# Moving the sums, weightings, selects and score transpositions of a graph attention kernel to other steps of its order

## The chip, the cores and the metric

The kernel runs on one core of a Trainium2 chip. The metric is the time of one execution on the device, in microseconds (us). The time before the change is 5646.86 us, the median of three runs between 5633.02 and 5650.22 us. The traced execution is a run of its own with its own time.

## The reference

One layer of attention over a graph with 12500 nodes and 412500 edges, with a softmax over all edges and two layer norms behind it. Cut to what matters:

```python
h = x @ Wn + bn; q = x @ Wq + bq; k = x @ Wk + bk; v = x @ Wv + bv
eh = edge_attr_64 @ We + be
attn_in = concatenate([q[src], k[dst], eh], axis=-1)
hmid = leaky_relu(attn_in @ A1 + b1, 0.2)
scores = leaky_relu(hmid @ A2 + b2, 0.2)          # 8 heads
w = softmax(scores.mean(axis=-1), axis=0)         # over all edges
out = segment_sum(w[:, None] * v[dst], src, num_segments=12500)
y = gamma * layernorm(h + out) + beta
result = layernorm(x + y)
```

The edges come sorted by `dst`. The sums go by `src`, which is in no order.

## The kernel before

The first layer is folded into the tables, so that an edge's hidden row is a sum of a part by its `dst`, a part by its edge features and a part by its `src`. The work is in two halves that run at the same time for most of the kernel.

The first half, `make`, goes through 403 groups of 1024 edges in the order of `dst`. In each group PE makes the rows of all edges with one-hot matrices (`rows`, L932 and L939), ACT copies them out of PSUM (`evacuate`, L950 and L951), and POOL scatters them with indirect DMAs (L962) into a table in HBM that is sorted by blocks of `src`. DVE makes the one-hots (L852 to L872) and, with counts from PE (L881), the places of the rows (L902 to L915). Each group is cut into six pieces by `yield`.

The second half, `sums_of`, takes the table back in units of up to four blocks, at most 16 tiles of 128 edges. For each unit SP loads rows into `rt` (L1146, six buffers), PE transposes them and adds the `src` part (`hidden`, L1236 and L1246, one call for four tiles), ACT copies the result out of its bank (`copied`, L1257) and DVE makes the leaky Relu (`leaky`, L1261). PE multiplies by A2 (`scores`, L1272), ACT applies a Relu to z (`above_zero`, L1286), and PE transposes z (`heads`, L1298, the score transpositions). DVE adds the heads and takes maxima (`maxima`, from L1314), PE transposes the maximum (`maximum`, L1331), and DVE makes the reference of the softmax from it (`reference`, L1340 and L1341). ACT takes the exponentials (`weights`, L1350). For each four tiles DVE then makes one-hot selects (`select`, L1359, two buffers), ACT multiplies them by the weights (`weigh`, L1373, three buffers), and PE sums the rows with them (`add`, L1406, one PSUM bank `psm`). DVE adds the sum to the earlier one (`total`, L1423; L1416 in the first part), which SP had loaded (`before_it`, L1383), and SP stores it (`store`, L1435).

`hidden`, `scores` and `rows` take their banks from one ring of five PSUM banks (`bank`).

The order is written out by hand. `lags` gives each operation of a unit a step, counted from the unit's own start. A new unit starts every eight steps, so several units are in flight, and an operation at step 20 of one unit stands in the same step as one at step 12 of the next. `do` puts an operation into its step; within a step the calls stand in the order of the units, and those with `late=1` come last. `load_at` of the rows follows from `lead`, and from the last step of `add` of the unit that had the buffer before. The steps are emitted between the pieces of `make`; once no group is left, the steps that remain, those of the last units and of the closing norms, run alone. Each engine runs its own instructions in the order in which they are emitted, and waits by semaphores for the others.

Of the kernel before, what the change touches and what calls it, by code (L numbers as in the profile page):

```python
# [478 lines left out]
def sorted_path(  # L479
# [258 lines left out]
    above = const.tile([P, P], BF)  # L738
# [23 lines left out]
    late = {}  # L762
# [338 lines left out]
    def lags(p):  # L1101

        return dict(
            every=EVERY, lead=25 if p == NR - 1 else 19, sources=-13, turned=-12, spread=-7, q=-7,
            onehot=-2, copied=2, leaky=4, scores=12, above=14, heads=15, maxima=17, maximum=18,
            reference=20, weights=21, old=16, lowered=24, select=(19, 21, 23, 25),
            weigh=(21, 23, 25, 27), add=(24, 25, 27, 28), total=30, store=33,
        )

    def sums_of(bp):  # L1110


        plans, s0, free, starts, ends = [], 19, ([], []), {}, {}
        for p, bs, t in units:
            nt = len(bs) * t
            nk = -(-nt // 4)
            o = lags(p)
            if plans:
                s0 += plans[-1][4]["every"]


            mine = free[spare_buffer(len(plans))]
            held = MORE if mine is free[1] else BLKS
            load_at = mine[-held] + 1 if len(mine) >= held else 0
            s0 = max(s0, load_at + o["lead"] - 1)
            if plans:
                s0 = max(s0, plans[-1][2] + EVERY)
            if plans:
                s0 += (plans[0][2] - s0) % EVERY
            load_at = max(load_at, s0 - o["lead"])  # L1130
            mine.append(s0 + o["add"][-1])
            starts.setdefault(p, load_at)
            ends[p] = load_at
            plans.append((nt, nk, s0, load_at, o))
        steps = {}

        def do(step, fn, *args, late=0):
            steps.setdefault(max(int(step // 1), 0), []).append((late + step % 1, fn, args))
# [300 lines left out]
        def pieces(i):  # L1439
            at = list(range(0, plans[i][0], 4)) + [plans[i][0]]  # L1440
            return list(zip(at[:-1], at[1:]))

        for i, (nt, nk, s0, load_at, o) in enumerate(plans):
            do(load_at, load, i)
            do(s0 + o["sources"], sources, i)
            do(s0 + o["turned"], turned, i)
            do(s0 + o["turned"], put, i)
            do(s0 + o["spread"], spread, i)
            do(s0 + o["q"], load_q, i)
            for k, (c, c1) in enumerate(pieces(i)):  # L1450
                n, s = c1 - c, s0 + 2 * k
                t = units[i][2]
                for u in range(-(-c // t), (c1 - 1) // t + 1):
                    do(s + o["onehot"], onehot, i, u)
                do(s, hidden, i, c, c, n, k)
                do(s + o["copied"], copied, i, c, c, n, k, late=1)
                do(s + o["leaky"], leaky, i, c, c, n, k, late=1)
            do(s0 + o["scores"], scores, i, 0, nt)
            do(s0 + o["above"], above_zero, i)
            do(s0 + o["heads"], heads, i, 0, nt)  # L1460
            do(s0 + o["maxima"], maxima, i)
            do(s0 + o["maximum"], maximum, i, late=1)
            do(s0 + o["reference"], reference, i)
            do(s0 + o["weights"], weights, i)
            do(s0 + o["old"], before_it, i)
            do(s0 + o["lowered"], lowered, i)
            for j, t0 in enumerate(range(0, nt, 4)):
                n = min(4, nt - t0)
                if t0 % SEL == 0:
                    m = min(SEL, nt - t0)  # L1470
                    do(s0 + o["select"][j], select, i, t0, m)
                do(s0 + o["weigh"][j], weigh, i, t0, n)
                do(s0 + o["add"][j], add, i, t0, n)
            do(s0 + o["total"], total, i)
            do(s0 + o["store"], store, i)
# [350 lines left out]
    with tc.manual_schedule():  # L1826
# [6 lines left out]
        tabs, made, nt = tables(), 0, 1 + (2 * ng - 1) * (10 + 6) + ng  # L1833
        more, sent, ne = later(), 0, 11 * (len(chunks) - 1)
        done, r = 0, 0
        for i, _ in enumerate(_ for p in range(NP) for _ in make(p)):
            while fills and fills[-1][0] <= i:
                fill_piece(*fills.pop()[1])
            while made < nt and made * n0 < i * nt:
                next(tabs, None)  # L1840
                made += 1
            while sent < ne and sent * n0 < i * ne:
                next(more, None)
                sent += 1
            if i == n1:
                for _ in tabs:
                    pass
                for _ in more:
                    pass
                spans()  # L1850
                covered()
                tab_pool.close()
                steps, starts = sums_of(pool("blk", BLKS))
            if i < n1:
                continue
            while r + 1 < NR and i >= 6 * begun[r + 1]:
                r += 1
            if r + 1 < NR:
                until = starts[r] + (starts[r + 1] - starts[r]) * (i - 6 * begun[r]) / (
                    6 * (begun[r + 1] - begun[r])  # L1860
                )
                while done < until:
                    for fn, args in steps[done]:
                        fn(*args)
                    done += 1
# [86 lines left out]
```

## Time and profile before

| | |
|---|---|
| median of three runs | 5646.86 us |
| traced execution | 5660.61 us, span 5658.8 us |
| PE busy | 4277.5 us (76%) |
| DVE busy | 4078.5 us (72%) |
| POOL busy | 3455.8 us (61%) |
| ACT busy | 3104.1 us (55%) |
| moved by DMA | 1486.96 MB, 263 GB/s |
| mean granted TensorE clock | 0.832 |

PEld is the load of weights into PE, which runs beside its matmuls. "Issue" as the end of a wait means that the trace shows nothing that the engine waited for, "remote" that a semaphore was raised by something that the trace doesn't tell. An arrow says what ended a wait: "PE psS L1298 <- ACT z L1286" is PE, idle ahead of its transpositions at line 1298, until ACT's z of line 1286 was done. The ends of matmuls are modelled.

### The profile page before, as it was taken

The numbers are of one execution on the slowest core, as the hardware profiler recorded it, in microseconds if no ns is written. First come the engines' busy times: TensorE is split into PE (matmuls) and PEld (weight loads), VectorE is DVE, ScalarE is ACT, GpSimd is POOL, SyncE is SP. The second block draws the span as 40 slices with busy tenths as digits, with TensorE's granted clock in tenths as the row PEclk, the third lists the DMA queues.
The fourth block names the chain that finished last, engine by engine and source line by source line (L and its number), as shares of the span: only waits on it lengthen the run. The fifth ranks groups of instructions, "written<-read, shape, count | busy, mean of one in ns | idle before, by whom it ended". The sixth has DMA issues, their size and how long they took to land. (4 is left out here: it accounts for less than half of the span.)

```text
span 5658.8 us, 89624 instructions
## 1 busy us (share of the span) xinstructions
PE 4277.5 (76%) x28928; PEld 3043.3 (54%) x28928; DVE 4078.5 (72%) x8952; ACT 3104.1 (55%) x8846; POOL 3455.8 (61%) x3277
## 2 busy tenths in 40 slices
PE   4545536777778877778788887888777787888897
PEld 2333324555555565555555565656555555555677
DVE  7867745666667777767677777777777777776787
ACT  2432224444556566555555665666655666555786
POOL 4776666666666655666666666666556666666113
PEclk6766657778888888888888988888888889888999
DMA  6877866677777788877778888788887888887985
GB/s 189 275 255 255 251 221 207 225 236 233 242 267 275 261 276 270 263 273 257 263 267 283 293 270 289 274 273 272 273 266 268 271 283 275 272 276 254 351 318 188
DMA packets 727112, 1486.96 MB, mean 263 GB/s; under 512 B 157377, under 2 KB 326356, under 8 KB 724839
## 3 DMA queue, kind: packets, MB, share of 16 engines
q1 hardware_dynamic: 535538, 1055.66, 57.1%
q0 software_dynamic: 154752, 424.43, 20.5%
q10 hardware_dynamic: 36340, 1.05, 0.4%
q8 instruction: 229, 3.75, 0.3%
q14 instruction: 253, 2.06, 0.1%
HBM read 901.45 MB, written 579.32 MB: 262 GB/s over the span
## 5 line engine op out<-in xcount | busy, mean ns | idle before, releaser
L962 POOL DMA_INDIRECT rtab<-rec,idx x3224 | 3371.3, 1046 | 1866.2 <-issue 860.4
L950 ACT ACTIVATE rec<-bank 128x512 f32<-128x512 f32 x1612 | 882.5, 594 | 1195.3 <-remote 404.6
L1406 PE MATMUL psm<-rt,ohw 128*128 128x128 f32 x7448 | 1211.4, 307 | 158.3 <-issue 145.5
L1373 ACT ACTIVATE ohw<-ohs,w 128x128 f32<-128x128 bf16 x3724 | 1217.4, 403 | 44.9 <-DVE ohs L1359 17.9
L1406 PEld LDWEIGHTS psm<-rt,ohw 128*128 128x128 f32 x7448 | 1064.5, 215 | 238.8 <-issue 189.1
L1257 ACT ACTIVATE hm<-bank 128x512 f32<-128x512 f32 x932 | 550.7, 591 | 569.6 <-remote 125.5
L939 PE MATMUL bank<-WeS,eat 64*128 64x128 f32 x6448 | 748.4, 335 | 117.7 <-issue 113.9
L932 PE MATMUL bank<-kvs,ohd 128*128 128x256 bf16 x3224 | 591.1, 302 | 260.4 <-ACT rec L950 121.1
L902 DVE TENSOR_TENSOR ats<-pc,oh 128x792 f32<-128x792 f32 x403 | 393.0, 975 | 528.0 <-remote 235.3
L1236 PE MATMUL bank<-ident,rt 128*128 128x128 f32 x3724 | 673.7, 302 | 90.2 <-issue 85.9
L939 PEld LDWEIGHTS bank<-WeS,eat 64*128 64x128 f32 x6448 | 540.7, 216 | 357.6 <-issue 350.3
L1236 PEld LDWEIGHTS bank<-ident,rt 128*128 128x128 f32 x3724 | 467.8, 154 | 370.5 <-issue 282.6
L1246 PE MATMUL bank<-ohT,qs 128*128 128x512 bf16 (+3 forms) x2156 | 622.1, 380 | 57.5 <-issue 43.4
L1224 DVE TENSOR_SCALAR ohT<-rowB,iotaP,power 128x512 bf16<-128x512 uint8 (+1 forms) x980 | 563.4, 578 | 138.4 <-remote 47.1
L1261 DVE SCALAR_TENSOR_TENSOR hm<-hm 128x512 f32<-128x512 f32 x932 | 636.4, 683 | 3.5 <-ACT hm L1257 2.3
L872 DVE TENSOR_SCALAR ohd<-dstb,node 128x1152 bf16<-128x1152 uint8 x404 | 566.1, 1401 | 26.5 <-remote 19.4
L932 PEld LDWEIGHTS <-ohd 128*128 128x128 bf16 x3224 | 333.2, 107 | 440.7 <-issue 345.1
L1359 DVE TENSOR_TENSOR ohs<-iotaE,sl 128x512 bf16<-128x512 bf16 x932 | 394.4, 423 | 34.6 <-ACT ohw L1373 27.1
L1272 PE MATMUL bank<-hm,A2s 128*32 128x512 f32 x1864 | 385.4, 687 | 31.4 <-issue 22.3
L913 DVE TENSOR_REDUCE pos<-ats 128x8 f32<-128x792 f32 x403 | 390.1, 968 | 2.6
L1286 ACT ACTIVATE z<-bank,b_c 128x512 f32<-128x512 f32 (+3 forms) x252 | 170.7, 677 | 336.4 <-remote 224.8
L1298 PE MATMUL psS<-ident,z 128*128 128x128 f32 (+2 forms) x1000 | 183.7, 315 | 200.3 <-ACT z L1286 194.5
(198 smaller groups left out, 3760.7 us busy)
## 6 DMA issues: line engine op xcount, KB each, us to landing
rt<-rtab SPq DMA_DIRECT2D x192, 2056.0 KB
eat<-in_ea SPq DMA_DIRECT2D x201, 512.0 KB
rt<-rtab SPq DMA_DIRECT2D x48, 1542.0 KB
qs<-qtab SPq DMA_DIRECT2D x240, 256.0 KB
atab<-old SPq DMA_DIRECT2D x240, 256.0 KB
old<-atab SPq DMA_DIRECT2D x216, 256.0 KB
rtab<-rec,idx POOLq DMA_INDIRECT x3224
dstb<-dtab SPq DMA_DIRECT2D x201, 256.0 KB
```

The source lines that it names most:

```text
L872: nc.vector.tensor_scalar(to, row[:, cols], node, None, op0=ALU.is_equal)
L932: nc.tensor.matmul(pk[h][:, i, :], ohd[h * (GT // 2) + j + i], kvs, start=(i == 0), stop=False,)
L939: nc.tensor.matmul(pk[h][:, i, :D], eat[half, (j + i) * P : (j + i + 1) * P], WeS[half, :], start=False, stop=(i == 1),)
L950: nc.scalar.activation(rec[:, h, :, : 2 * D], pk[h], AF.Copy)
L962: one_tile = nc.gpsimd.indirect_dma_start(out=rtab[:, :], out_offset=bass.IndirectOffsetOnAxis(ap=idxs[g][:, t : t + 1], axis=0), in_=rec[ ...
L1224: nc.vector.tensor_scalar(st["oh"][u][:, : t * P].rearrange("p (t q e) -> p t q e", q=4, e=32), st["rowB"][:, : nt * P] .rearrange("p (q t ...
L1236: nc.tensor.matmul(ph[:, j * P : (j + 1) * P], st["rt"][:, t0 + j, :D], ident, is_transpose=True, start=(j == 0), stop=False,)
L1246: nc.tensor.matmul(ph[:, cols], st["qs"][:, u, s, :], st["oh"][u][:, (j0 - u * t) * P : (j1 - u * t) * P], start=False, stop=(s == 1 and j ...
L1257: nc.scalar.activation(hm, state[i].pop(("ph", k))[:, : n * P], AF.Copy)
L1261: nc.vector.scalar_tensor_tensor(hm, hm, SLOPE, hm, op0=ALU.mult, op1=ALU.max)
L1373: nc.scalar.activation(ohw[:, j, :], ohs[:, :, t0 % SEL + j], AF.Copy, scale=st["w"][:, t0 + j : t0 + j + 1])
L1406: nc.tensor.matmul(st["psm"][:, u * P : (u + 1) * P], ohw[:, j, :], st["rt"][:, t0 + j, D : 2 * D], start=(k == 0), stop=(k == t - 1),)
```

## The change

Only steps are changed; every operation stays as it is, and the same instructions are issued.

```diff
-            onehot=-2, copied=2, leaky=4, scores=12, above=14, heads=15, maxima=17, maximum=18,
-            reference=20, weights=21, old=16, lowered=24, select=(19, 21, 23, 25),
-            weigh=(21, 23, 25, 27), add=(24, 25, 27, 28), total=30, store=33,
+            onehot=-2, copied=2, leaky=4, scores=11, above=13, heads=15, maxima=17, maximum=18,
+            reference=20, weights=21, old=15, lowered=24, select=(19, 20, 22, 23),
+            weigh=(21, 22, 24, 25), add=(23, 25, 26, 27), total=29, store=32,
...
-            do(s0 + o["heads"], heads, i, 0, nt)
+            do(s0 + o["heads"], heads, i, 0, nt, late=1)
```

Scores, Relu, old sums, totals and stores go one step forward. The second select and weighting go one step forward, the third one, the last two. Of the sums the first, third and fourth go one step forward and the second stays. The transpositions stay in their step but come last in it.

What that does to the order of PE shows in the middle of the program, behind the last `hidden` of a unit. Before:

```order
L1246 MATMUL bank_41595<-ohT_41528,qs_41201 128x512
L1298 MATMUL psS_41614<-ident_81,z_41593 128x128 x4
L881 LDWEIGHTS above_276
L881 MATMUL pc_33945<-few_41588,above_276 128x99
L881 LDWEIGHTS above_276
L881 MATMUL pc_33945<-few_41588,above_276 128x99
L1406 MATMUL psm_41638<-rt_40365,ohw_41540 128x128 x4
L1236 MATMUL bank_41645<-ident_81,rt_41076 128x128 x4
```

With the change, at the same place:

```order
L1246 MATMUL bank_41602<-ohT_41530,qs_41206 128x512
L1406 MATMUL psm_41614<-rt_40368,ohw_41543 128x128 x4
L1298 MATMUL psS_41623<-ident_81,z_41548 128x128 x4
L881 LDWEIGHTS above_276
L881 MATMUL pc_33947<-few_41591,above_276 128x99
L881 LDWEIGHTS above_276
L881 MATMUL pc_33947<-few_41591,above_276 128x99
L1236 MATMUL bank_41653<-ident_81,rt_41079 128x128 x4
```

The first sum of the unit before (L1406, the first to write its `psm`) stood behind the transpositions (L1298) and the counts of `make`, and stands ahead of them now.

On ACT, around the weights of one unit and the Relu z of the next. Before:

```order
L1350 ACTIVATE w_28354,sums_353<-S_28232,ref_351 128x16
L1373 ACTIVATE ohw_28356<-ohs_28277,w_28354 128x128 x4
L950 ACTIVATE rec_28365<-bank_28306 128x2x256
L950 ACTIVATE rec_28365<-bank_28307 128x2x256
L951 ACTIVATE rec_28365<-srcl_210 128x4
L1286 ACTIVATE z_28380<-bank_28333,b2_c_110 128x512
L1257 ACTIVATE hm_28345<-bank_28338 128x512
L1373 ACTIVATE ohw_28406<-ohs_28361,w_28354 128x128 x4
```

With the change:

```order
L1350 ACTIVATE w_28357,sums_353<-S_28237,ref_351 128x16
L1373 ACTIVATE ohw_28359<-ohs_28281,w_28357 128x128 x4
L1286 ACTIVATE z_28364<-bank_28283,b2_c_110 128x512
L950 ACTIVATE rec_28368<-bank_28315 128x2x256
L950 ACTIVATE rec_28368<-bank_28316 128x2x256
L951 ACTIVATE rec_28368<-srcl_210 128x4
L1373 ACTIVATE ohw_28382<-ohs_28338,w_28357 128x128 x4
L1257 ACTIVATE hm_28347<-bank_28340 128x512
```

The Relu moved past the copies of a record, and the second weighting (the second L1373) past the copy of a hidden bank (L1257).

On DVE, from the reference of a unit on. Before:

```order
L1341 SCALAR_TENSOR_TENSOR ref_351<-m1_44432,ref_351 128x1
L1261 SCALAR_TENSOR_TENSOR hm_44340<-hm_44340 128x512
L1359 TENSOR_TENSOR ohs_44462<-iotaE_88,sl_43613 128x512
L852 TENSOR_TENSOR oh_44485<-blk_209,iotaE_88 128x792
L862 TENSOR_TENSOR both_44487<-oh_44485 128x396
L864 TENSOR_TENSOR few_44489<-both_44487 128x198
L872 TENSOR_SCALAR ohd_44491<-dstb_43913,node_269 128x3x384
L1423 SCALAR_TENSOR_TENSOR old_44136<-old_44136,by_44321,psm_44324 128x512
L1224 TENSOR_SCALAR ohT_44496<-rowB_44375,iotaP_90,power_206 128x384
L1224 TENSOR_SCALAR ohT_44498<-rowB_44375,iotaP_90,power_206 128x384
L1261 SCALAR_TENSOR_TENSOR hm_44398<-hm_44398 128x512
L1359 TENSOR_TENSOR ohs_44507<-iotaE_88,sl_43613 128x512
```

With the change:

```order
L1341 SCALAR_TENSOR_TENSOR ref_351<-m1_44436,ref_351 128x1
L1359 TENSOR_TENSOR ohs_44439<-iotaE_88,sl_43617 128x512
L1261 SCALAR_TENSOR_TENSOR hm_44346<-hm_44346 128x512
L1423 SCALAR_TENSOR_TENSOR old_44128<-old_44128,by_44329,psm_44316 128x512
L852 TENSOR_TENSOR oh_44488<-blk_209,iotaE_88 128x792
L862 TENSOR_TENSOR both_44490<-oh_44488 128x396
L864 TENSOR_TENSOR few_44492<-both_44490 128x198
L872 TENSOR_SCALAR ohd_44494<-dstb_43920,node_269 128x3x384
L1359 TENSOR_TENSOR ohs_44501<-iotaE_88,sl_43617 128x512
L1224 TENSOR_SCALAR ohT_44503<-rowB_44375,iotaP_90,power_206 128x384
L1224 TENSOR_SCALAR ohT_44505<-rowB_44375,iotaP_90,power_206 128x384
L1261 SCALAR_TENSOR_TENSOR hm_44402<-hm_44402 128x512
```

The second select (the first L1359) moved past a leaky Relu (L1261), the total (L1423) past the one-hots of a record group (L852 to L872), and the third select past two one-hots (L1224) and a leaky Relu.

## The prediction

> **What bounds the kernel now.** I read the page first, then busy time by stage, then who waits for whom inside the long middle stage, and last the instructions of one disturbed and one smooth stretch in order of time. The stages (busy us and instructions of PE, PEld, DVE, ACT and POOL, then granted clock, DMA share, GB/s):
>
> ```profile
> span 5658.8 us, 89624 instructions
> ...
> 0.00:900.00 900.00, 450.64 (x2473) 302.52 (x2473) 619.11 (x1074) 261.68 (x504) 590.72 (x570) 0.66 0.75 239
> 900.00:5190.00 4290.00, 3429.71 (x23469) 2423.71 (x23469) 3104.54 (x6817) 2492.36 (x7285) 2749.29 (x2636) 0.85 0.79 266
> 5190.00:5659.00 469.00, 397.10 (x2998) 317.07 (x2994) 354.89 (x1062) 350.05 (x1059) 115.75 (x73) 0.96 0.76 281
> ```
>
> The middle stage, where records are made and summed at once, is 4290 of 5659 us, and no engine fills it: PE is busy for 80% of it and DVE for 72%. In the tail PE is busy for 85%, ahead of DVE and ACT. The waits of the middle stage on PE, in us, times and longest, and one of DVE:
>
> ```profile
> PE psS L1298 <- ACT z L1286: 183.3, 88, 6.9
> PE psm L1406 <- issue: 144.6, 268, 1.5
> PE bank L939 <- issue: 112.0, 196, 1.3
> PE bank L1236 <- issue: 72.5, 136, 1.7
> PE bank L932 <- issue: 69.0, 101, 3.2
> PE bank L932 <- ACT rec L950: 51.7, 36, 5.4
> ...
> PE psm L1406 <- DVE old L1423: 4.1, 5, 1.3
> ...
> PE psm L1406 <- ACT ohw L1373: 3.2, 6, 0.9
> ...
> DVE ohs L1359 <- ACT ohw L1373: 16.6, 27, 1.4
> ```
>
> The largest single wait of PE is for the Relu z, ahead of the score transpositions (L1298): 88 times, 2.1 us each on average. Sums never wait for their weightings to speak of (3.2 us), so starting the weightings sooner can save nothing by itself. The four "issue" rows, 398 us, have no releaser and nothing in the change touches them. Now a disturbed stretch and the smooth one behind it, first by busy time of the same engines, then by instruction:
>
> ```profile
> 3490.00:3500.00 10.00, 2.97 (x18) 1.70 (x17) 2.29 (x5) 1.64 (x5) 6.24 (x7) 0.89 0.53 155
> 3500.00:3510.00 10.00, 9.56 (x69) 8.48 (x73) 9.76 (x25) 9.20 (x29) 4.76 (x4) 0.77 0.95 352
> 3510.00:3520.00 10.00, 10.00 (x89) 7.35 (x90) 9.83 (x22) 8.88 (x26) 8.17 (x7) 1.00 0.90 297
> ```
>
> ```profile
> 3487.24 1.06 PE L1272 MATMUL bank<-hm,A2s 128*32 128x512 f32 x8
> ...
> 3499.70 0.69 ACT L1286 ACTIVATE z<-bank,b_c 128x512 f32<-128x512 f32 x1 [7.17 <-remote]
> ...
> 3500.44 1.11 PE L1298 MATMUL psS<-ident,z 128*128 128x128 f32 x4 [3.37 <-ACT z L1286]
> ...
> 3508.50 0.16 DVE L1341 SCALAR_TENSOR_TENSOR ref<-m,ref 128x1 f32<-128x1 f32 x1
> ...
> 3509.55 0.30 ACT L1350 ACTIVATE w<-S,ref 128x16 f32<-128x16 f32 x1
> ...
> 3509.90 1.06 PE L1272 MATMUL bank<-hm,A2s 128*32 128x512 f32 x8
> 3509.97 1.33 ACT L1373 ACTIVATE ohw<-ohs,w 128x128 f32<-128x128 bf16 x4
> ...
> 3510.87 0.73 DVE L1423 SCALAR_TENSOR_TENSOR old<-old,by,psm 128x512 f32<-128x512 f32 x1
> ...
> 3511.21 0.66 ACT L1286 ACTIVATE z<-bank,b_c 128x512 f32<-128x512 f32 x1
> ...
> 3515.20 0.61 PE L1298 MATMUL psS<-ident,z 128*128 128x128 f32 x4
> ...
> 3515.65 1.06 PE L1406 MATMUL psm<-rt,ohw 128*128 128x128 f32 x8
> ...
> 3516.17 0.42 DVE L1359 TENSOR_TENSOR ohs<-iotaE,sl 128x512 bf16<-128x512 bf16 x1
> ...
> 3522.55 1.07 PE L1272 MATMUL bank<-hm,A2s 128*32 128x512 f32 x8
> ```
>
> The kernel runs in two modes. Undisturbed, a unit of eight steps takes 3522.55 - 3509.90 = 12.65 us with PE and DVE both full, and the transpositions find z ready 3.3 us early. Disturbed, DVE and ACT stand still for want of PE's results: the scores' matmuls at 3487.24 show an end at 3488.3, but z starts only at 3499.70 although ACT had been idle for 7.17 us, and PE, having done what it could, stands before the transpositions for 3.37 us. The waits for z belong to the second mode.
>
> **The change part by part.** Nothing is added or removed; work is moved.
>
> *The first sum ahead of the transpositions.* A sum of four tiles (1.06 us, row 3515.65) now stands before the transpositions and not behind them. When PE must wait for z, it does this sum first, if the partial sums' bank is free, and that seldom fails (L1406 <- DVE old, 4.1 us). Upper bound: 88 x 1.06 = 93 us. Lower bound: nothing, where another engine decides. Right after the wait at 3500.44 DVE is busy for 9.76 and 9.83 of 10 us, so a microsecond that PE saves there need not move the end; elsewhere PE is the fuller one. I take a third of the bound, -31 us. Between the scores and the transpositions nothing else is gained: scores and Relu both go one step forward, so that ACT gets z in the same order behind the first weighting.
>
> *The tail.* The same wait there:
>
> ```profile
> PE psS L1298 <- ACT z L1286: 11.2, 21, 1.7
> ```
>
> Its mean of 0.53 us is below one sum of 1.06 us, so nearly all of it is covered; at most -11.2 us. PE is the fullest engine there and I take -8.
>
> *Selects nearer to the weightings.* There are two select buffers, and the third and fourth select now follow the first and second weighting by one step instead of two. In the smooth stretch the reference ends at 3508.66 on DVE, and the first weighting on ACT at 3511.30. Behind the reference DVE would do a select (0.42), a total (0.73), and the one-hot and leaky Relu of
>
> ```profile
> 3508.58 0.54 DVE L1224 TENSOR_SCALAR ohT<-rowB,iotaP,power 128x512 bf16<-128x512 uint8 x1
> ...
> 3509.04 0.68 DVE L1261 SCALAR_TENSOR_TENSOR hm<-hm 128x512 f32<-128x512 f32 x1
> ```
>
> together 2.4 us, to 3511.0: without record work between, DVE stands for 0.3 us. Today's wait is 16.6 us in 27 waits, 0.61 each. Bounds: 0, and two selects in each of 220 units at 0.61, +268 us of DVE. I take three times today's, +33 us on DVE, a third of it on the path: +11 us.
>
> *The copy behind the second weighting.* The middle stage has 220 units, and 2632 / 8 = 329 groups of records:
>
> ```profile
> L932 PE MATMUL bank<-kvs,ohd 128*128 128x256 bf16 x2632 | 461.5, 292 | 148.1 <-issue 69.0 <-ACT rec L950 51.7 <-ACT hm L1257 11.6
> ...
> L1286 ACT ACTIVATE z<-bank,b_c 128x512 f32<-128x512 f32 (+2 forms) x220 | 149.1, 678 | 326.5 <-remote 224.8 <-PE bank L1246 51.2 <-PE bank L939 23.6
> ```
>
> On ACT the weights and first weighting (3509.55 to 3511.30), the Relu (0.66) and the second weighting (1.33) now follow each other, 3.7 us ahead of a copy that gives back one of five PSUM banks. One copy gets a weighting of 1.33 us ahead of it, another loses one. Bounds: +293 us, if all 220 units pay one weighting, and -63 us, if all that PE waits at L932 for record and hidden copies today (51.7 and 11.6) went. I take 0, between them, since the weightings ahead of copies are as many as before.
>
> *Totals, stores and loads.* Total, store and the load of the old sums move with the sums by one step. The total passes record work on DVE in some places, and it waits for a sum that moved as far; I take 0. On SP the order of row loads, stores and spreads stays, only record loads pass them. The place of the row load in the program does not move, and its buffer comes free at the same place of PE's order (the last sum stands just before the scores in both). 0, and the wait of the sums for rows, which the rows above do not show, stays hidden.
>
> Sum: -31 - 8 + 11 = -28 us. The profiled execution took 5660.6 us, its span 5658.8 and 1.8 around it; 5660.6 - 28 = 5632.6. It lies 13.7 us above the median of the runs, 5646.9, so for a median I predict 5646.9 - 28 = **5619 us**.
>
> **The rivals.**
>
> *No change.* The wait for z is a symptom: PE's late results hold up every engine, and when PE has done its sum it waits as long for the next thing that ACT or DVE has not done, since both resume only when the results arrive. For it: z at 3499.70 started 11.4 us after the recorded end of the scores, and one sum is 1.06 us. Against it: 88 waits of 2.1 us are twice a sum, not ten times. It leaves the tail's part and part of the select's cost, about -2: 5645 us. The Trainium skill, "Perfetto Trace Analysis", section "Summary: the profiler window per engine type", says that the end shown for TensorE is an estimate and that semaphore propagation lies outside the window; the 11.4 us between scores and z agree that the shown end is not when the consumer is let go.
>
> *Slower: ACT's burst holds the banks.* The 3.7 us of weights, weighting, Relu and weighting, and a record copy when one falls in, stand ahead of a copy of a hidden bank. A unit takes four hidden banks, one for scores and, with 1.5 groups of four, six for records; in a smooth stretch PE then asks for one every 12.65 / 11 = 1.15 us, five last for 5.8 us, and PE stands before L932 or L1236. If half of the 220 units lose half a weighting, 0.66 us, that is +73 on the path less the 39 saved: 5647 + 34 = 5681 us. It decides from the point where PE's waits for ACT at those lines rise by over 39 us. For it: ACT fills 8.88 and 9.20 of 10 us in smooth stretches. Against it: three of four copies stand behind a weighting today as well.
>
> *Faster still: the clock.* The clock drops when PE stands:
>
> ```profile
> 3497.00:3499.00 2.00, 0.07 (x1) 0.00 (x0) 0.56 (x2) 0.00 (x0) 1.01 (x1) 0.70 0.95 238
> 3499.00:3501.00 2.00, 0.56 (x3) 0.56 (x4) 1.15 (x2) 1.30 (x3) 0.00 (x0) 0.50 0.96 356
> 3501.00:3505.00 4.00, 4.00 (x20) 3.63 (x19) 3.83 (x12) 3.97 (x14) 0.67 (x1) 0.55 1.02 408
> ```
>
> Of 6 us after that wait, PE ran at about half its clock, some 2.7 us lost. If the sum that fills the wait keeps the clock up in 20 of the 88 cases, 54 us more are saved: 5619 - 54 = 5565 us. The Trainium skill, "TensorE: Matmul & The Clock Gate", section "What's actually happening", has the clock halve after an idle window of about 3.4 us; the 0.50 behind 3.37 us of waiting agrees. Against it: a pause that comes from late results is as long with the sum done first, only 1.06 us of it is filled.
>
> **How the numbers follow.** Forecast 0.38 (its own range 5595 to 5632), no change 0.30, slower 0.20, clock 0.12. The range for 8 in 10 reaches below to the clock's 5565, with a little of the 93 us bound beyond it, and above past the slower rival's 5681: 5558 to 5692. This kernel's runs tell 0.3% from no change, 17 us: faster is under 5630, slower over 5664. The clock and nearly all of the forecast are faster, 0.48; no change and the forecast's upper edge 0.31; the slower rival with a little of the upper edge of no change 0.21.
>
> **What would show it.** In the changed kernel's waits of 900 to 5190 us, L1298 <- z should fall from 183 us to some 100, and in the tail from 11 to under 3. L1359 <- ohw on DVE should rise from 16.6 to about 50; over 100 would say that the selects cost more than I gave them. L932 and L1236 <- ACT should stay near 64 us; 39 more and the slower rival is right. If z's wait falls but the time stays and waits at other lines of PE or the "issue" rows rise by as much, it was a symptom. If z's wait does not fall at all, the step about the first sum is wrong.

## The result, and the profile after

The changed kernel takes 5691.66 us (median of five runs, 5683.19 to 5708.17) against 5646.86 us of the kernel before (now five runs, the same median): a ratio of 1.0088, 95% interval 1.0064 to 1.0113. It is slower by 45 us between the medians, where a time 28 us shorter was forecast. The profiled execution has a span of 5689.9 us against 5658.8, 31 us more.

Busy time by stage in the profile after (us of the stretch, busy us and instructions of PE, PEld, DVE, ACT and POOL, granted clock, DMA share, GB/s):

```profile
span 5689.9 us, 89962 instructions
...
900.00:5190.00 4290.00, 3427.59 (x23402) 2411.20 (x23402) 3099.62 (x6798) 2468.35 (x7261) 2728.90 (x2630) 0.86 0.80 265
```

In the same 4290 us PE issues 23402 matmuls where it issued 23469, 0.3% fewer, and it stands for 862.4 us where it stood for 860.3. DVE stands for 1190.4, before 1185.5. So the idle time in these 4290 us is what it was, though the 0.3% of work not done in them would take some 12 us more. The waits are not what they were. Two rows of PE before that the prediction doesn't show, from 900 to 5190 us, in us, times and longest:

```profile
PE bank L932 <- ACT hm L1257: 11.6, 9, 2.3
PE bank L932 <- ACT z L1286: 8.7, 3, 3.7
```

After:

```profile
PE psS L1298 <- ACT z L1286: 1.7, 2, 0.8
...
PE bank L932 <- ACT z L1286: 74.8, 46, 5.5
PE bank L932 <- ACT rec L950: 68.4, 35, 5.8
PE bank L932 <- ACT hm L1257: 21.2, 21, 3.1
...
DVE ohs L1359 <- ACT ohw L1373: 132.9, 91, 5.8
```

The wait for z ahead of the transpositions, 183.3 us before, is gone. PE now stands at the next thing that it needs from ACT, the banks at L932 (z 8.7 to 74.8 us, records 51.7 to 68.4, hidden copies 11.6 to 21.2), and DVE stands at its selects (16.6 to 132.9). On DVE the groups of two lines show the same shift (busy us and mean ns, then idle time ahead of them and what ended it). Before, then after:

```profile
L902 DVE TENSOR_TENSOR ats<-pc,oh 128x792 f32<-128x792 f32 x330 | 321.9, 976 | 417.5 <-remote 167.9 <-PE psm L1406 53.6 <-PE psS L1298 44.6
...
L1340 DVE TENSOR_REDUCE m<-psS 128x1 f32<-128x128 f32 x218 | 61.0, 280 | 273.1 <-PE psm L1406 128.3 <-remote 65.6 <-PE bank L1272 29.0
```

```profile
L902 DVE TENSOR_TENSOR ats<-pc,oh 128x792 f32<-128x792 f32 x328 | 319.9, 975 | 306.8 <-remote 128.4 <-PE bank L939 47.6 <-PE psm L1406 35.7
...
L1340 DVE TENSOR_REDUCE m<-psS 128x1 f32<-128x128 f32 x216 | 61.0, 282 | 396.8 <-remote 105.3 <-PE bank L939 64.5 <-PE bank L1272 54.8
```

DVE waits 111 us less for the counts of the records and 124 us more for the maximum. From the 60th to the last group of records, by the places that DVE makes at L913, the two traces differ by 16 us (4451.0 and 4467.0). That is about half of the 31 us between the two spans, and single traces don't tell whether it is the change.

The tail is another matter, and has the other half. Its 25 units, the last part (from the weights, L1350, of unit 225 to those of unit 249), before and after:

```profile
5299.00:5524.00 225.00, 208.62 (x1588) 158.31 (x1587) 185.14 (x481) 198.44 (x612) 25.53 (x12) 1.00 0.89 331
```

```profile
5313.00:5554.00 241.00, 217.50 (x1588) 169.13 (x1586) 188.76 (x480) 198.32 (x612) 25.35 (x12) 0.99 0.87 308
```

The same instructions and the same 74 MB (331 GB/s in 225 us, 308 in 241) take 16 us longer, with no engine nearer to being full. What differs is SP. Its waits from 5300 to 5550 us, before and after:

```profile
SPq L1383 <- DMA atab<-old: 25.8, 15, 3.6
SPq L1383 <- DMA row<-slT: 25.8, 6, 5.5
SPq L1146 <- DMA rt<-rtab: 9.9, 5, 3.0
```

```profile
SPq L1383 <- DMA atab<-old: 104.8, 22, 7.8
```

SP waits 104.8 us for stores of the sums to land before it may load the next old sums (L1383) into their buffer, of which there are three. What stands behind that load shows in SP's instructions in order of time (start, duration, line). Before:

```profile
5386.56 0.42 SPq L1146 DMA_DIRECT2D rt<-rtab  x1
5393.19 0.33 SPq L1496 DMA_DIRECT2D end<-in_x  x1
5393.63 0.38 SPq L1383 DMA_DIRECT2D old<-atab  x1
5394.05 0.43 SPq L1435 DMA_DIRECT2D atab<-old  x1
5394.52 0.43 SPq L1214 DMA_DIRECT2D rowB<-row  x1
5395.05 0.62 SPq L1172 DMA_DIRECT2D qs<-qtab  x1
5395.72 0.70 SPq L1146 DMA_DIRECT2D rt<-rtab  x1
```

After:

```profile
5402.65 0.32 SPq L1504 DMA_DIRECT2D xtab<-end  x1
5408.36 0.32 SPq L1383 DMA_DIRECT2D old<-atab  x1
5408.73 0.43 SPq L1146 DMA_DIRECT2D rt<-rtab  x1
5409.97 0.33 SPq L1496 DMA_DIRECT2D end<-in_x  x1
5410.35 1.54 SPq L1435 DMA_DIRECT2D atab<-old  x1
5411.94 0.45 SPq L1214 DMA_DIRECT2D rowB<-row  x1
5412.49 0.51 SPq L1172 DMA_DIRECT2D qs<-qtab  x1
5420.92 0.32 SPq L1383 DMA_DIRECT2D old<-atab  x1
5421.30 0.43 SPq L1146 DMA_DIRECT2D rt<-rtab  x1
```

Before, the row load of 2 MB (L1146) is issued, and the load of the old sums waits behind it, with the rows under way. After, the load of the old sums stands ahead of the row load: SP stops from 5403.0 to 5408.4, and from 5413.0 to 5420.9, and only then issues the rows. The loads of `qs` and `rowB` come later too, and PE in the tail now waits for `qs` (L1246 on PEld, 3.8 us before):

```profile
PEld L1246 <- DMA qs<-qtab: 20.5, 14, 3.8
PE bank L1246 <- DVE ohT L1224: 12.8, 7, 3.9
```

The table of lags says why the order turned over. In the last part the row load's lead is 25, so it falls into step 7 of eight; `old` at 16 fell into step 0 behind it, and `old` at 15 falls into the same step 7, where an older unit's calls stand first. In the other parts the lead is 19.

### The profile page after: what moved, and what is told of

Same layout as the page of the kernel before. It is cut to its first block, busy times and chain, and to the rows that moved or that the text cites. A ratio compares the mean times of both kernels' runs of the same rounds, so it can differ in the third digit from the quotient of the medians.

```text
span 5689.9 us, 89962 instructions
## 1 busy us (share of the span) xinstructions
PE 4298.5 (76%) x28928; PEld 3048.2 (54%) x28928; DVE 4090.9 (72%) x8952; ACT 3086.9 (54%) x8846; POOL 3439.6 (60%) x3277
## 3 DMA queue, kind: packets, MB, share of 16 engines
q8 instruction: 229, 3.75, 0.3%
## 5 line engine op out<-in xcount | busy, mean ns | idle before, releaser
L950 ACT ACTIVATE rec<-bank 128x512 f32<-128x512 f32 x1612 | 879.5, 593 | 1212.8 <-remote 364.8
L1406 PE MATMUL psm<-rt,ohw 128*128 128x128 f32 x7448 | 1220.2, 309 | 210.6 <-issue 163.0
L1373 ACT ACTIVATE ohw<-ohs,w 128x128 f32<-128x128 bf16 x3724 | 1214.1, 399 | 75.3 <-remote 43.5
L1406 PEld LDWEIGHTS psm<-rt,ohw 128*128 128x128 f32 x7448 | 1072.9, 214 | 339.6 <-issue 254.6
L932 PE MATMUL bank<-kvs,ohd 128*128 128x256 bf16 x3224 | 609.9, 305 | 372.4 <-ACT rec L950 144.1
L1257 ACT ACTIVATE hm<-bank 128x512 f32<-128x512 f32 x932 | 546.8, 587 | 591.3 <-remote 212.4
L939 PE MATMUL bank<-WeS,eat 64*128 64x128 f32 x6448 | 730.5, 335 | 90.8 <-issue 87.8
L1246 PE MATMUL bank<-ohT,qs 128*128 128x512 bf16 (+3 forms) x2156 | 628.9, 381 | 107.0 <-issue 56.6
L932 PEld LDWEIGHTS <-ohd 128*128 128x128 bf16 x3224 | 330.1, 108 | 645.7 <-issue 543.6
L1261 DVE SCALAR_TENSOR_TENSOR hm<-hm 128x512 f32<-128x512 f32 x932 | 636.6, 683 | 10.4 <-ACT hm L1257 4.5
L1224 DVE TENSOR_SCALAR ohT<-rowB,iotaP,power 128x512 bf16<-128x512 uint8 (+1 forms) x980 | 572.7, 588 | 69.3 <-DMA rowB<-row 40.2
L872 DVE TENSOR_SCALAR ohd<-dstb,node 128x1152 bf16<-128x1152 uint8 x404 | 566.1, 1401 | 23.0 <-remote 11.4
L1359 DVE TENSOR_TENSOR ohs<-iotaE,sl 128x512 bf16<-128x512 bf16 x932 | 393.2, 422 | 188.2 <-ACT ohw L1373 157.7
L913 DVE TENSOR_REDUCE pos<-ats 128x8 f32<-128x792 f32 x403 | 390.1, 968 | 2.9
L1340 DVE TENSOR_REDUCE m<-psS 128x1 f32<-128x128 f32 x250 | 70.0, 280 | 412.6 <-remote 112.9
L1246 PEld LDWEIGHTS <-qs 128*128 128x128 f16 x2156 | 219.5, 105 | 169.1 <-issue 119.4
```

The source lines that it names most:

```text
L872: nc.vector.tensor_scalar(to, row[:, cols], node, None, op0=ALU.is_equal)
L932: nc.tensor.matmul(pk[h][:, i, :], ohd[h * (GT // 2) + j + i], kvs, start=(i == 0), stop=False,)
L939: nc.tensor.matmul(pk[h][:, i, :D], eat[half, (j + i) * P : (j + i + 1) * P], WeS[half, :], start=False, stop=(i == 1),)
L950: nc.scalar.activation(rec[:, h, :, : 2 * D], pk[h], AF.Copy)
L1224: nc.vector.tensor_scalar(st["oh"][u][:, : t * P].rearrange("p (t q e) -> p t q e", q=4, e=32), st["rowB"][:, : nt * P] .rearrange("p (q t ...
L1246: nc.tensor.matmul(ph[:, cols], st["qs"][:, u, s, :], st["oh"][u][:, (j0 - u * t) * P : (j1 - u * t) * P], start=False, stop=(s == 1 and j ...
```

## The experiments

Two kinds of chips were met: on three chips the kernel before takes 5647 (the first result), 5735 and 5741 us, on three others 4886, 4890 and 4888. Each ratio is to the kernel before on the same chip, with its 95% interval; the first and second kind are called slow and fast kind below. The theories by their letters, where the expectations use letters: S, the selects wait for their two buffers; B, scores and Relu hold banks and z longer; H, the first sum ahead of the transpositions delays them; O, the load of the old sums ahead of the row load; M, the third sum, now ahead of hidden and of the maximum's transposition, delays the reference.

### Each part alone

**Selects and weightings alone**, on the kernel before:

```diff
-            reference=20, weights=21, old=16, lowered=24, select=(19, 21, 23, 25),
-            weigh=(21, 23, 25, 27), add=(24, 25, 27, 28), total=30, store=33,
+            reference=20, weights=21, old=16, lowered=24, select=(19, 20, 22, 23),
+            weigh=(21, 22, 24, 25), add=(24, 25, 27, 28), total=30, store=33,
```

> The kernel before, with the selects at 19, 20, 22, 23 and the weightings at 21, 22, 24, 25, everything else as before. Theory S (the third and fourth select stand on DVE for one of two select buffers, until the first and second weighting are done): the wait of L1359 for L1373 on DVE rises from 17 us to 100 to 140 us in the middle stage and the time from 5647 to between 5665 and 5690 us. Theory B (the scores' bank is held for longer, PE stands at L932 for z) and theory H (the transpositions and the maximum come one sum later, DVE stands for them): the select's wait may rise, but the time stays within 5637 to 5657 us.

1.0005 (0.9989 to 1.0021). The selects' wait rose from 16.6 us (on the first chip) to 62.9, less than theory S said, and it costs nothing that can be told.

**Scores and Relu alone** (`scores=11, above=13`):

> The kernel before, with the scores at step 11 and the Relu at 13, everything else as before. Theory B: the wait of L932 for z rises from 9 us to 60 to 80 us and the time to between 5665 and 5690 us. Theories S and H: the wait for z ahead of L1298 stays near 180 us or falls, and the time stays within 5635 to 5657 us.

0.9993 (0.9977 to 1.0009). The wait for z ahead of the transpositions fell to 81.4 us, the one at L932 rose from 8.7 to 19.7, the time stayed.

**The first sum alone**, ahead of the transpositions:

```diff
-            weigh=(21, 23, 25, 27), add=(24, 25, 27, 28), total=30, store=33,
+            weigh=(21, 23, 25, 27), add=(23, 25, 27, 28), total=30, store=33,
...
-            do(s0 + o["heads"], heads, i, 0, nt)
+            do(s0 + o["heads"], heads, i, 0, nt, late=1)
```

> The kernel before, with the first sum at step 23 and the transpositions last in their step, everything else as before. Theory H: the waits of DVE ahead of L1314 and L1340 rise by 100 to 200 us together and the time to between 5665 and 5690 us. Theories S and B, with the prediction's first step: the wait of L1298 for z falls from 183 to about 100 us, and the time to between 5610 and 5640 us.

0.9989 (0.9975 to 1.0004), with a wait for z of 16.2 us: it fell further than expected, and the time less. The edit that takes nine tenths of the wait away is worth 6 us of 5735 at its best guess, and nothing for certain. The waits of theory H rose by 74 us together, less than its 100 (ahead of L1314 from 50.4 to 151.3, ahead of L1340 from 273.1 to 246.4, against the trace of the first chip), and its loss isn't there.

**Three select buffers in the changed kernel** (a small tile of the closing norms goes into a weighting's buffer to make room; the same holds for the run called "best try" below):

```diff
-    selp = pool("sel", 2)
+    selp = pool("sel", 3)
...
-                    else scp.tile([P, 2, 10 * NB], FP, name="sm")
+                    else ohwp.tile([P, 4, P], FP, name="ohw")
```

> The changed kernel with three select buffers instead of two (room for the third is made by putting a small tile of the closing norms into a buffer of the weighted selects, which are free by then). Theory S: the wait of L1359 for L1373 falls from 136 us to under 20 us and the time from 5692 to between 5630 and 5660 us. Theories B and H: the wait falls as well, but the time stays at 5675 to 5700 us, and the waits of L1340 and L1314 on DVE and of L932 for z on PE stay as they are.

1.0058 (1.0038 to 1.0079): no better than the changed kernel on that kind of chip (1.0048, next). The selects' wait from 900 to 5190 us is as good as gone,

```profile
DVE ohs L1359 <- ACT ohw L1373: 5.3, 6, 1.6
```

from 132.9 us, and nothing is gained. S, B and H each fall as the cause of the loss.

### Putting parts of the change back

**The changed kernel unchanged**, as the measure for the next three:

> The changed kernel once more, on the chip of the next three, as their measure. Theory O (the load of the old sums passed the row load on the SP queue in the tail, waits there for the store of the unit three before, and holds up the row load) and theory M (the third sum, now ahead of hidden and maximum, delays the maximum, and DVE stands for it) both expect 1.006 to 1.010 of the kernel before, with the last 25 units at some 240 us.

1.0048 (1.0030 to 1.0067), below the 1.006 that was expected at the least; the last 25 units take 243.1 us, and SP waits 129.2 us at L1383 in the tail.

**Only the load of the old sums back** (`old=15` to `old=16`):

> The changed kernel with the load of the old sums back at step 16, so that it stands behind the row load in the tail again. Theory O: SP's wait of L1383 for the store falls from 105 us to under 30 us, the last 25 units from 241 us to 223 to 229 us, the ratio by 0.002 to 0.003 below that of the changed kernel. Theory M, and theory S (selects on two buffers): no change of the ratio beyond 0.001, the tail stays near 240 us.

1.0012 (0.9996 to 1.0028), an interval wholly below that of the changed kernel. Its last 25 units, and SP's wait in the tail:

```profile
5379.00:5604.00 225.00, 212.69 (x1565) 167.62 (x1586) 188.27 (x479) 197.22 (x612) 26.12 (x12) 1.00 0.90 331
```

```profile
SPq L1383 <- DMA atab<-old: 4.4, 1, 4.4
```

225 us again, at 331 GB/s. This one number carries 0.0036 of the 0.0048, some 21 us, of which the tail shows 18.

**The old sums, the last three sums, total and store back** (`old=16`, `add=(23, 25, 27, 28)`, `total=30`, `store=33`):

> The changed kernel with the third and fourth sum back at 27 and 28, total at 30, store at 33 and the load of the old sums at 16. Theory M, on top of what the old load gives: DVE's waits ahead of L1340 fall by 100 us or more, and the ratio falls by a further 0.003 to 0.005, to within 0.002 of the kernel before. Theory S: L1340 may wait less, but the time is that of the run with the old load alone put back.

0.9986 (0.9973 to 0.9998). Against the run before it DVE's wait for the maximum falls to some half. There, and here:

```profile
L1340 DVE TENSOR_REDUCE m<-psS 128x1 f32<-128x128 f32 x214 | 60.8, 284 | 472.9 <-remote 159.5 <-PE bank L939 119.0 <-PE bank L1272 52.0
```

```profile
L1340 DVE TENSOR_REDUCE m<-psS 128x1 f32<-128x128 f32 x214 | 59.7, 279 | 255.5 <-remote 91.1 <-PE bank L939 56.3 <-PE bank L1272 39.6
```

The difference, 0.0026 or 15 us, is less than the 0.003 that theory M expected, and at the edge of what these runs tell: the two intervals just touch (0.9996 and 0.9998). That the halved wait is what saves it isn't shown: the trace with it is an execution of 5752.43 us, longer than the other's 5741.86.

**The old sums, scores and Relu back** (`old=16`, `scores=12`, `above=14`):

> The changed kernel with the scores back at 12, the Relu at 14 and the load of the old sums at 16. Theory B (PE stands at L932 for the bank that z still has, now that scores and Relu come a step earlier): L932's wait for z falls from 75 us to under 20 us and the ratio by 0.003 to 0.005 below the run with the old load alone put back. Theories M and S: the same time as that run within 0.001, with PE standing for z elsewhere.

0.9996 (0.9979 to 1.0013), beside 1.0012 with only the old sums back. The wait at L932 for z is 5.5 us again, and the time is not told apart.

### Wait or symptom, and the old sums alone

**The load of the old sums one step forward, alone**, on the kernel before (`old=16` to `old=15`):

> The kernel before with one number of the change: the loads of the old sums go one step forward (old 16 to 15), so that in the tail each stands ahead of the row load on SP instead of behind it; nothing else moves. Theory O (on SP the waiting load of the old sums holds up the row load behind it, and this is most of the loss): the last 25 units take about 240 us instead of 224, SP's wait at L1383 in the tail rises from some 25 us to over 100, ratio 1.002 to 1.004. Rival (the loss needs the other moves of the change too, for instance totals and stores that come at another place): the tail stays within 3 us of 224 and the ratio within 0.999 to 1.001.

1.0016 (1.0001 to 1.0031), below the 1.002 that was expected at the least, though its interval holds the 0.0023 that the tail's 13 us come to. The tail is as theory O has it:

```profile
5371.00:5609.00 238.00, 210.13 (x1567) 161.21 (x1587) 186.85 (x480) 198.83 (x613) 25.32 (x12) 0.99 0.87 310
```

```profile
SPq L1383 <- DMA atab<-old: 121.4, 25, 9.0
```

238 us at 310 GB/s, where the next three runs on the same chip, with `old` at 16, take 225.0 to 226.3.

**The three moves of the forecast's saving alone** (`scores=11, above=13`, first sum at 23, transpositions last):

> The kernel before with the three moves on which the prediction's saving rests: scores and Relu one step forward, the first sum one step forward, the transpositions last in their step. Old sums, selects, weightings, the other sums, totals and stores stay. Prediction's first-sum step: the wait for z ahead of L1298 falls from 183 us to under 50 and the time by 31 us or more, ratio 0.995 or less. Theory of the symptom (PE's late results hold up every engine; PE only waits at another line): the wait falls as much, the idle time of PE between 900 and 5190 us stays within 15 us, ratio 0.998 to 1.001.

0.9979 (0.9967 to 0.9991): faster by 12 us. **The transpositions one step earlier** (`heads=15` to `heads=14`), which takes cover away from the wait:

> The kernel before with the transpositions of z one step earlier (heads 15 to 14), so that PE has one hidden bank of some 1.25 us less, in some units a record as well, between scores and transpositions. It enlarges the wait that the prediction wanted to remove. If PE's wait for z is on the path: it grows from 183 us by at least 88 x 1.25 = 110 us, and the time by as much or a third of it, +37 to +110 us, ratio 1.006 to 1.02. If it is a symptom: the wait grows as much, waits at other lines fall by as much, and the ratio stays within 0.998 to 1.003.

1.0049 (1.0031 to 1.0068): slower by 28 us. The wait from 900 to 5190 us in the run with the saving, and in the one with less cover (the first row is the run before them, on the same chip, which leaves both in place):

```profile
PE psS L1298 <- ACT z L1286: 171.9, 90, 5.5
```

```profile
PE psS L1298 <- ACT z L1286: 5.8, 4, 2.1
```

```profile
PE psS L1298 <- ACT z L1286: 411.0, 142, 12.9
```

166 us less of waiting save 12 us, 239 us more cost 28 (by the ratio; the run is a scattered one, 5744 to 5803 us, and its median is 17 us longer). So about a tenth of this wait is time: by the two intervals 3 to 11% and 7 to 16%. PE's idle time from 900 to 5190 us went the same way, from 954 us in the run before them to 919 and 1004, where the theory of the symptom had it stay within 15 in the first. Both runs lie between the two theories' numbers, the first by 0.0001: the wait is mostly a symptom, and not wholly.

**Best try** (the run with old and late sums back, with a third select buffer):

> The change with the load of the old sums, the last three sums, the total and the store back at their places before, and a third select buffer (paid for with a small tile of the closing norms, which goes into a weighting's buffer). If the waits of the selects for their buffers cost time once the rest is put back: ratio 0.996 or less. If they are idle time that goes elsewhere, as with three buffers in the changed kernel: the same as without the third buffer, 0.9986, within 0.0015.

0.9995 (0.9979 to 1.0012), within the 0.0015: a third buffer brings nothing here either.

### The order of the two loads, and the other kind of chip

**The load of the old sums last in its step**, in the changed kernel: still one step earlier than before, but behind the row load.

```diff
-            do(s0 + o["old"], before_it, i)
+            do(s0 + o["old"], before_it, i, late=1)
```

> The changed kernel, with the loads of the old sums last in their step: still one step earlier than before, but in the tail behind the row load of the same step on SP instead of ahead of it. Theory O (what costs is that the waiting load of the old sums stands ahead of the row load): the last 25 units take some 225 us again instead of 241, SP's wait at L1383 falls from over 100 us to under 30, and the ratio is that of the run with old at its former step, 1.0012, within 0.0015. Rival (what costs is that the old sums are loaded one step too early, before the store that frees their buffer, wherever they stand): SP's wait stays over 60 us, the tail over 235 us, and the ratio within 0.0015 of the changed kernel's 1.0048.

0.9968 (0.9943 to 0.9993), on a chip of the fast kind, so that the numbers of the expectation, which are from the slow kind, don't apply to the ratio. They do to the tail: 224.9 us, and SP's wait at L1383 is 25.3 us. So the earlier step does no harm; standing ahead of the row load does. **The changed kernel, and the same swap, on one chip** of the fast kind:

> The changed kernel as it is, beside the next two on one chip: the run with old behind the row load fell on a chip on which the kernel before takes 4886 us, so it can't be compared with the changed kernel's 1.0048 or 1.0088 from other chips. Theory O: about 16 us of the tail are lost, so the ratio lies 0.003 above that of the next run, and the last 25 units take about 240 us. If the chip is one of the slower two kinds, 1.005 to 1.009.

> The changed kernel with the loads of the old sums last in their step, on the same chip as the run before it. Theory O: tail 225 us, ratio 0.003 (0.0015 to 0.005) below the changed kernel's. Rival (the row load's place is not what costs): the same ratio as the changed kernel's within 0.0015.

1.0007 (0.9997 to 1.0018) for the changed kernel, 0.9964 (0.9949 to 0.9980) with the loads in the old order: 0.0043, or 19 us apart, and the tails 241.8 and 224.2 us. SP's wait in the tail, in the one and the other:

```profile
SPq L1383 <- DMA atab<-old: 104.5, 22, 7.6
```

```profile
SPq L1383 <- DMA atab<-old: 25.6, 14, 4.6
```

Theory O stands on both kinds, with the tail 12 to 18 us longer wherever that order is (238 to 243 us in the five traces with it, 224 to 228 in the others).

**The last sums, total and store alone**, on the kernel before (`add=(24, 25, 26, 27), total=29, store=32`), on the fast kind:

> The kernel before with the last moves alone: third and fourth sum, total and store one step forward (add 24, 25, 26, 27; total 29; store 32). Theory M (the third sum ahead of hidden and of the maximum's transposition delays the reference and holds DVE up): DVE's idle time ahead of the references, L1340, rises by 100 us or more from the 273 us of before, ratio 1.001 to 1.003. Rival (it was scatter between two runs, or needs the selects' moves too): ratio 0.999 to 1.001.

1.0021 (1.0011 to 1.0031). The time is as expected, the trace is not: DVE's idle time ahead of L1340 is only 33.8 us there. What shows is a wait of PE, from 900 to 4450 us,

```profile
PE psm L1406 <- ACT ohw L1373: 160.5, 123, 4.5
```

since the last two sums come one step nearer to weightings that stay. In the full change the weightings move too, and the wait is 20.2 us on that kind of chip. So this run has a cost of its own, and says nothing of theory M.

**The three moves of the saving again**, on the fast kind:

> The three moves of the prediction's saving alone (scores, Relu and first sum one step forward, transpositions last in their step), again beside the others: it was 0.9979 on a chip where the kernel before takes 5741 us. If that is what these moves are worth: 0.9965 to 0.999 here, and below the run with old behind the row load, which also has the late sums one step forward (1.0021 alone) and the selects.

1.0008 (0.9996 to 1.0020): a miss. What saved 12 us on the slow kind saves nothing there.

**The run with old and late sums back, again**, on the fast kind:

> The changed kernel with the load of the old sums, the last three sums, total and store at their steps before; what is left of the change are scores, Relu, first sum, transpositions, selects and weightings. On a chip of the second kind (kernel before some 5740 us) it was 0.9986. If the late sums cost on every chip what they cost alone (1.0021), on the fast kind (kernel before some 4890 us) it should lie 0.002 below the run with old behind the row load, 0.9964: 0.993 to 0.996. Rival (on the fast kind it is the scatter that sets the time, and the sums' places are worth nothing): 0.996 to 0.998 there.

0.9957 (0.9942 to 0.9972), 4865.39 us. It is faster than the kernel before on both kinds (0.9986 on the slow one), and the best version found. The late sums are not told apart here: 0.9964 with them, 0.9957 without, where 0.002 were expected if they cost what they cost alone. Against the three moves alone (1.0008) it has the earlier selects and weightings besides; so these seem worth 0.005 on the fast kind and nothing on the slow one (0.9986 against 0.9979), each time by a difference between two chips of the kind. Which wait that gain comes from was not tried; ACT's wait for the scatter ahead of the record copies (L950) is 741.5 us in the trace of the three moves and 524.9 here.

## Why the prediction was wrong

- **Totals, stores and loads: 0. This step failed.** It said that on SP "the order of row loads, stores and spreads stays, only record loads pass them". The load of the old sums was listed as moving one step, and its place against the row load was not looked at in the last part, where the lead is another. It passes the row load there, waits for its buffer, and holds the rows up: 16 us of the traced tail, 0.0036 of the time on the slow kind (1.0048 to 1.0012) and 0.0043 on the fast one (1.0007 to 0.9964). On the second chip it decides the sign: without it the ratio is 1.0012, no change that can be told. On the first chip 16 to 21 us are less than half of the 45. In the same step the totals and late sums were put at 0; with them back the ratio is 0.9986, so they may cost some 15 us on the slow kind. By what wait is open.
- **The first sum ahead of the transpositions: -31.** Size wrong, sign right on the slow kind. The wait fell further than forecast, to 1.7 us instead of some 100, and by more than the bound of 93 us. Two moves work on it, where the step counted one: it said that with scores and Relu both a step forward nothing else is gained, but alone they bring the wait to 81.4 us. And the sum alone brings it to 16.2, so the bound itself was too low. It took a sum of the smooth stretch, 1.06 us; the sum right behind the disturbed stretch's wait (L1406 at 3501.35) takes 1.91 us, at a granted clock of 0.55. Whether that is the whole difference isn't shown. On the path the step failed the other way: it took a third of what the sum covers as saved, and the 12 us measured for these moves are 7% of the wait taken away. The rival "no change" had the mechanism for the most part: PE, with its sum done, stands at the next line. Its sign, waits at other lines rising by as much, is what the trace of the middle stage shows. Of the 11.4 us that the prediction counts there between the scores and z, ACT stood for 7.17; until 3492.5 it had the copies of a record to do. About a tenth of the wait is time all the same, as the two runs with more and less cover show.
- **The tail: -8.** The wait fell as said, from 11.2 us to less than 1, but with the loads in the old order the tail of the runs with that move takes 224 to 228 us, before 225: nothing arrives.
- **Selects nearer to the weightings: +11.** The wait is 132.9 us, not 50, which the forecast called a sign that the selects cost more. They don't: alone they are 1.0005, and taking the wait away gains nothing. The term should have been about 0 on the slow kind. On the fast kind the same moves seem to gain.
- **The copy behind the second weighting: 0**, and the rival "ACT's burst holds the banks". Waits at L932 for ACT rose by 92 us with those for z, 26 without, and the rival's time, 5681, is near the result. So the result lies just inside the upper end of the stated range, 5692, but that end was set for this rival, and its cause isn't what happened: weightings and selects alone are 1.0005, scores and Relu alone 0.9993.
- **The clock**, a rival for a faster time, did not rise: 0.837 in the profiled execution and 0.831 or 0.832 in the other four, before 0.832. Its price was read too high as well. The granted clock is 0.90 from 3497 to 3498 us and 0.50 in the next microsecond, so it fell early in the 3.37 us of waiting, which begin at 3497.1, and was not brought down by their length; PE had been busy for only 0.50 and 0.19 us of the two microseconds ahead of them. And 1.4 of the 6 us that were counted lie within the wait, so that only some 4 us of work ran at half the clock.

On the second chip, taking parts back one after another divides the +28 us into +21 for the old sums' load, +15 for the late sums and -8 for the rest. Such steps add up by their making, and moves that were run alone give less: +9 us for the old sums' load (1.0016), -12 for the three moves, +3 for selects and weightings; the late sums were not run alone on the slow kind. What the moves cost together beyond that stays open. By the steps of taking back, of the 73 us between forecast and result 36 are the step that failed (21 and 15) and 20 a saving that came out as 8 instead of 28 us. The remaining 17 are what the first chip's 45 us are above the second's 28. The first chip's interval (1.0064 to 1.0113) only touches that of the second (1.0030 to 1.0067), and what more was lost there stays open, since no part was run on it.

## What to carry to other kernels

Where one queue issues in order, ask of every load that moves which loads it passes in each stage of the program, and which of them must wait: a small load that waits for its buffer, put ahead of a large one, costs the large one its start. A wait of the fullest engine is not time until taking cover away, or adding some, has moved the end; it can move to the next line instead. The idle time summed over the stage is a better measure than the single wait, and still not the time: it fell by 35 us where the time fell by 12.

## What was not expected of the hardware

The same program takes 5647 to 5741 us on some chips and 4886 to 4890 on others, and the waits differ in kind. The changed kernel from 900 to 4450 us, on the first chip and on one of the fast kind:

```profile
900.00:4450.00 3550.00, 2825.49 (x19327) 1998.76 (x19326) 2565.75 (x5632) 2034.47 (x5980) 2256.32 (x2178) 0.85 0.80 264
```

```profile
900.00:4450.00 3550.00, 2961.35 (x23317) 2211.93 (x23315) 3054.06 (x6775) 2444.72 (x7251) 2728.17 (x2605) 0.93 0.94 318
```

The fast one issues 21% more matmuls in the same time. ACT's largest wait for something that the trace doesn't name, on the first chip, and on the fast one ACT's largest wait of all:

```profile
ACT rec L950 <- remote: 259.3, 77, 8.8
```

```profile
ACT rec L950 <- DMA rtab<-rec,idx: 680.6, 319, 7.3
```

On the fast kind these "remote" waits are as good as gone from the list, and the scatter's transfers hold up the record copies instead. So what the prediction read as PE's late results is there on one kind of chip and not on the other, with the same program; that fits moves which save 12 us on the one kind and nothing on the other. What makes the results late was not found: the larger of two instruction queues shows 229 packets and 3.75 MB in both traces.
